# Layers 2 and 3 of a four-layer network on one core: columns in natural order, one load per pair half, six input and output buffers, rounding and residual copy on GpSimd

## The chip, the cores and the metric

The kernel runs on one core of one Trainium2 chip. The time is the device time of one execution in microseconds. A core has five engines with a queue of instructions each: PE multiplies matrices, DVE (VectorE), ACT (ScalarE) and POOL (GpSimd) work on tiles in the core's memory, and SP (SyncE) here only issues transfers. Each engine takes its instructions in a fixed order, and an instruction that waits holds up all that is behind it. Transfers between the chip's main memory and the core run on 16 DMA engines, whichever queue issues them. Matmul results arrive in PSUM, a second, small memory[...]. Tiles have 128 partitions.

## What is computed

The input x is (4, 8, 512, 512) in float32: 4 images, 8 channels, 512 rows, 512 columns. Four layers follow each other. Each normalizes x over groups of two channels and adds a function of the result to x:

```python
def _gn(v, G=4, eps=1e-5):          # mean and variance over 2 channels and all pixels
    ...
x = x + _L0_conv_ref(_gn(x), ...)   # spiking attention
x = x + _L1_conv_ref(_gn(x), w)     # 13 x 13 blur of each channel
x = x + _L2_conv_ref(_gn(x), weight, bias)
x = x + _L3_conv_ref(_gn(x), weight, bias)

def _L2_conv_ref(x, weight, bias):  # quantized 3 x 3 convolution over 8 channels
    sx = MAX_Q / jnp.max(jnp.abs(x))
    sw = MAX_Q / jnp.max(jnp.abs(weight))
    qx, qw = _quantize(x, sx), _quantize(weight, sw)     # round and clip to +-127
    out_i32 = lax.conv_general_dilated(qx, qw, ...)
    return out_i32 / (sx * sw) + bias[None, :, None, None]
```

Layer 3 is an ordinary float32 3 x 3 convolution over 8 channels with a bias. The change touches layers 2 and 3 alone.

## The kernel before

Layer 0 and layer 1 run first and take most of the time. Layer 1 leaves its result in main memory as `x2d[t]`, one array for each image t, with a row for each image row and channel. The columns of such a row don't lie in natural order there: they lie by phase, which means that column 4 v + g stands at place 128 g + v (`PH` = 4 phases, `NV` = 128 columns of each). The layers 2 and 3 of the kernel before keep this order to the end.

`layers23` works on windows of 8 image rows by 8 channels, 64 partitions each; a window advances by 6 rows. Two windows make a tile of 128 partitions by 512 columns (`windows(k)`), two tiles make a pair, and an image has 22 pairs, so 88 pairs in all. A 3 x 3 convolution is three matmuls for each window, one for each column offset dx; the rows and channels are in the band matrix. In the phase order, the neighbouring column of phase 3 is in phase 0 of the next v, so the tiles carry two more phases at their ends (`PH + 2`), which `outer_phases` fills by two shifted copies on POOL (L931, L932).

For a pair, `layer2` does this:
- `load(t, p)` (L936): four transfers of 128 KB on SP's queue, one for each window of each tile (L941), into a tile `x` out of a pool of four (L220). The loop asks for the load three pairs ahead (L1076).
- L951, ACT: y = x times scale plus bias, the normalization and the quantization scale.
- L956, DVE: rounding of y to whole numbers by adding and subtracting 12582912, written as bf16 to one of three tiles `xq`.
- L931 and L932, POOL: the outer phases of `xq`.
- L968, PE: 12 bf16 matmuls, 64 x 64 weights on 64 x 512 columns.
- L973, DVE: x3 = result times `inv` plus x (the residual, read from the loaded tile), into a ring `x3` of 24 pairs that stays in the core's memory; L976, DVE: its statistics.

After 11, 19 and 22 pairs of an image, `halos` copies border rows between windows inside `x3` (L993 on SP; L995 on SP, or on POOL's queue for the last chunk of an image). After 22 pairs `norm3` works out the normalization of layer 3 from the statistics: short DVE instructions, small matmuls and a power on POOL (L191).

`layer3` runs 23 pairs behind: L931 and L932 fill the outer phases of the pair in `x3`, L1039 (POOL) sets the two border columns, L1046 is 24 float32 matmuls, L1056 (ACT) adds the bias and writes the result `o` with the columns put back into natural order (it reads PSUM with a stride of 128 elements), into a pool of three. L1067 stores it, 192 KB: the first tile of a pair from ACT's queue, the second from POOL's.

The order within each queue comes from the framework's scheduler, which works at build time with estimated durations; `issue_after(did)` only asks that PE take a pair's layer 3 after the layer 2 of the current step. A pair's steps are thus not one after another: while PE works on one pair, ACT and DVE can be at later ones, as far as buffers (x 4, y 2, xq 3, PSUM 3 and 4, o 3) let them.

Of the kernel before, what the change touches and what calls it, by code (L numbers as in the profile page):

```python
# [42 lines left out]
P = 128  # L43
# [82 lines left out]
def network(ctx: ExitStack, tc: tile.TileContext, i: dict, out: bass.AP):  # L126
# [84 lines left out]
    def pool(name, bufs=1, **where):  # L211
# [5 lines left out]
    r2 = late.tile([P, T, G], F32, name="r2")  # L217
    most = late.tile([P, G], F32, name="most")
    early = {
        "x": ctx.enter_context(pool("x2", 4, side="right")),  # L220
        "y": ctx.enter_context(pool("y2", 2, side="right")),
        "o": ctx.enter_context(pool("o3", 3, side="right")),
    }
    with ExitStack() as s:
        ps_1 = s.enter_context(pool("ps_2", space=PSUM))
# [573 lines left out]
def weights23(tc, i, pool, scratch, ps_1, ident):  # L799


    nc = tc.nc

    def col(name, n=1):
        return pool.tile([P, n], F32, name=name)

    n_taps = 3 * B
    w = {}
    c24 = pool.tile([n_taps, i["c24"].shape[1]], F32, name="c24")
    nc.scalar.dma_start(c24, i["c24"])  # L810
    w2 = pool.tile([n_taps, n_taps], F32, name="w2t")
    nc.scalar.dma_start(w2, i["w2"])
    w3 = pool.tile([n_taps, n_taps], F32, name="w3t")
    nc.scalar.dma_start(w3, i["w3"])
    w["b2"], b3 = col("b2"), col("b3")
    nc.scalar.dma_start(w["b2"], i["b2"])
    nc.scalar.dma_start(b3, i["b3"])
    w["b23"] = col("b23")
    nc.vector.tensor_add(w["b23"], w["b2"], b3)

    def banded(taps, dtype, name, firsts):

        band = pool.tile([P, len(firsts), 3, HALF], dtype, name=name)
        for b, first in enumerate(firsts):
            ps = ps_1.tile([P, W_IN, n_taps], F32, tag="misc", name=f"ps_{name}")
            for row in range(W_IN):
                at = (W_IN - first - row) * B
                for a in range(2):
                    nc.tensor.matmul(
                        ps[a * HALF : (a + 1) * HALF, row, :], lhsT=c24[:, at : at + HALF],  # L830
                        rhs=taps, start=True, stop=True,
                    )
            for dx in range(3):
                nc.vector.tensor_copy(
                    band[:, b, dx, :].rearrange("p (r c) -> p r c", c=B),
                    ps[:, :, dx * B : (dx + 1) * B],
                )
        return band

    w["band3"] = band3 = banded(w3, F32, "band3", (-1, 1))
    w["sum3"] = pool.tile([P, 2, HALF], F32, name="sum3")
    nc.vector.tensor_add(w["sum3"], band3[:, :, 0, :], band3[:, :, 1, :])
    nc.vector.tensor_add(w["sum3"], w["sum3"], band3[:, :, 2, :])
    w["eye3"] = pool.tile([P, 2, 3, HALF], F32, name="eye3")
    nc.vector.memset(w["eye3"], 0.0)
    nc.vector.tensor_add(
        w["eye3"][:, 0, 1, B:], ident[:, : HALF - B], ident[:, HALF : P - B]
    )  # L850
    nc.vector.tensor_add(
        w["eye3"][:, 1, 1, : HALF - B], ident[:, B:HALF], ident[:, HALF + B :]
    )

    wall = scratch.tile([P, 2, D], F32, tag="y", name="wall")
    wall = wall.rearrange("p n d -> p (n d)")[:, : n_taps * n_taps]
    nc.scalar.dma_start(wall, bass.AP(i["w2"].tensor, 0, [[0, P], [1, n_taps * n_taps]]))
    w["sw"] = sw = col("sw")
    nc.vector.tensor_reduce(sw, wall, AX.X, ALU.max, apply_absolute_value=True)
    nc.vector.reciprocal(sw, sw)  # L860
    nc.vector.tensor_scalar_mul(sw, sw, MAX_Q)
    nc.vector.tensor_scalar_mul(w2, w2, sw[:n_taps])
    nc.vector.tensor_scalar(w2, w2, MAX_Q, -MAX_Q, op0=ALU.min, op1=ALU.max)
    nc.vector.tensor_scalar(w2, w2, ROUND, ROUND, op0=ALU.add, op1=ALU.subtract)
    w["band2"] = banded(w2, BF16, "band2", (0,))


    w["xq"] = [pool.tile([P, 2, PH + 2, NV], BF16, name=f"xq_{j}") for j in range(3)]
    for xq in w["xq"]:
        nc.gpsimd.memset(xq, 0.0)  # L870
    w["st3"] = [pool.tile([P, W2_N, 6], F32, name=f"st3_{j}") for j in range(2)]
    for st3 in w["st3"]:
        nc.gpsimd.memset(st3, 0.0)
    w["inv"] = col("inv")
    w["m"], w["r"] = col("m_own", T), col("r_own", T)
    w["mr"] = col("mr_own", T)
    return w


def layers23(  # L880
# [33 lines left out]
        w["mr"], w["m"], -1.0, w["r"], op0=ALU.mult, op1=ALU.mult  # L914
    )

    x3p = s.enter_context(pool("x3"))

    x3 = x3p.tile([P, 2 * RING, PH + 2, NV], F32, name="x3")
    flat = x3.rearrange("p n g v -> p n (g v)")  # L920
    last = (PH + 2) * NV - 1
    nc.gpsimd.memset(flat[:, :, 0 : last + 1 : last], 0.0)
    def tiles(p):
        return [k for k in (2 * p, 2 * p + 1) if k < W2_N]

    def slot(t, p):
        return 2 * ((t * N_PAIRS + p) % RING)

    def outer_phases(x):

        nc.gpsimd.tensor_copy(x[:, :, 0, 1:], x[:, :, PH, : NV - 1])  # L931
        nc.gpsimd.tensor_copy(x[:, :, PH + 1, : NV - 1], x[:, :, 1, 1:])  # L932

    ahead = {}

    def load(t, p):  # L936
        ahead[t, p] = xt = early["x"].tile([P, 2, D], F32, tag="x", name=f"x2_{t}_{p}")
        src = x2d[t]
        for j, k in enumerate(tiles(p)):
            for a, q in windows(k):  # L940
                nc.sync.dma_start(  # L941
                    xt[a * HALF : (a + 1) * HALF, j, :],
                    bass.AP(src.tensor, src.offset + q * W_STEP * B * D, [[D, HALF], [1, D]]),
                )

    def layer2(t, p):
        ks = tiles(p)
        n, n_p = len(ks), HALF * len(windows(ks[-1]))
        xt = ahead.pop((t, p))
        y = early["y"].tile([P, 2, D], F32, tag="y", name="y2")  # L950
        nc.scalar.activation(  # L951
            y[:n_p, :n, :], xt[:n_p, :n, :], AF.Identity, bias=w["mr"][:n_p, t : t + 1],
            scale=w["r"][:n_p, t : t + 1],
        )
        xq = w["xq"][(t * N_PAIRS + p) % 3][:n_p, :n]
        nc.vector.tensor_scalar(  # L956
            xq[:, :, 1 : PH + 1, :], y[:n_p, :n, :].rearrange("p n (g v) -> p n g v", g=PH),
            ROUND, ROUND, op0=ALU.add, op1=ALU.subtract,
        )
        outer_phases(xq)  # L960
        s0 = slot(t, p)
        st3 = w["st3"][t % 2]
        for j, k in enumerate(ks):
            ps = ps_2.tile([P, D], F32, tag="conv2", name="ps_conv2")
            for dx in range(3):
                for a, _ in windows(k):
                    half = slice(a * HALF, (a + 1) * HALF)
                    mm = nc.tensor.matmul(  # L968
                        ps[half, :], lhsT=w["band2"][half, 0, dx, :], rhs=xq[half, j, dx : dx + PH, :],
                        start=dx == 0, stop=dx == 2,  # L970
                    )
            own = x3[:n_p, s0 + j, 1 : PH + 1, :].rearrange("p g v -> p (g v)")
            nc.vector.scalar_tensor_tensor(  # L973
                own, ps[:n_p, :], w["inv"][:n_p], xt[:n_p, j, :], op0=ALU.mult, op1=ALU.add
            )
            nc.vector.bn_stats(st3[:n_p, k, :], own)  # L976
        return mm.ins

    pairs = flat[:, :, NV : (PH + 1) * NV].rearrange("p (n j) d -> p n j d", j=2)

    def halos(t, p0, p1):


        for c in range(4):
# [4 lines left out]
            for q0, q1, n_q in split(t, first, n, before - 1):  # L989
# [1 line left out]
                there = pairs[a_b * HALF : (a_b + 1) * HALF, q1 : q1 + n_q, j_b, :]  # L991
                end = (W_IN - 1) * B
                nc.sync.dma_start(here[:B], there[W_STEP * B : (W_STEP + 1) * B])  # L993
                engine = nc.gpsimd if p1 == N_PAIRS else nc.sync
                engine.dma_start(there[end : end + B], here[B : 2 * B])  # L995

    def split(t, p, n, back):

# [32 lines left out]
    def layer3(t, p, zero, band, const):  # L1031
# [2 lines left out]
        ks = tiles(p)  # L1034
        s0 = slot(t, p)
        n_p = HALF * len(windows(ks[-1]))
        outer_phases(x3[:n_p, s0 : s0 + len(ks)])
        edge = flat[:n_p, s0 : s0 + len(ks), 0 : last + 1 : last]
        nc.gpsimd.tensor_copy(edge, zero[:n_p].unsqueeze(2).to_broadcast([n_p, len(ks), 2]))  # L1039
        ps = [ps_3.tile([P, D], F32, tag="conv3", name="ps_conv3") for _ in ks]  # L1040
        for dx in range(3):
            for j, k in enumerate(ks):
                for a, q in windows(k):
# [1 line left out]
                    b = 1 if q == W_ALL - 1 else a ^ j  # L1045
                    nc.tensor.matmul(  # L1046
                        ps[j][b * HALF : (b + 1) * HALF, :], lhsT=band[half, b, dx, :],
                        rhs=x3[half, s0 + j, dx : dx + PH, :],
                        start=dx == 0, stop=dx == 2,
                    )  # L1050
        for j, k in enumerate(ks):
            q = 4 * p + 2 * j
            used = slice(HALF if q == W_ALL - 1 else 0, P)

            o = early["o"].tile([P, D], F32, tag="o", name="o3")
            nc.scalar.activation(  # L1056
                o[used].rearrange("p (v g) -> p v g", g=PH),
                ps[j][used].rearrange("p (g v) -> p v g", g=PH), AF.Identity, bias=const[used],
            )
            row, n = q * W_STEP + 1, 2 * W_STEP  # L1060
            at = 2 * B
            if q == 0:
                row, n, at = row - 1, n + 1, at - B
            if q == W_ALL - 1:
                n, at = W_STEP + 1, HALF
            engine = nc.gpsimd if j else nc.scalar
            engine.dma_start(  # L1067
                out[t, :, row : row + n, :].rearrange("c r w -> r c w"), o[at : at + n * B, :]
            )
# [3 lines left out]
    n_all = T * N_PAIRS  # L1073
    for n in range(n_all + N_PAIRS + 1):
        if n < n_all:
            for m in range(4) if n == 0 else [n + 3]:  # L1076
                if m < n_all:
                    load(*divmod(m, N_PAIRS))
            t, p = divmod(n, N_PAIRS)
# [47 lines left out]
```

## Time and profile before

| | us |
|---|---|
| median of 3 runs | 3185.09 |
| lowest and highest | 3183.04, 3185.96 |
| the profiled execution | 3180.31 |
| its span, first to last instruction | 3178.2 |
| layers 2 and 3 in it, from the first L951 at 2595.9 to the end | 582.3 |

All times of single steps come from the profiled execution. Over the whole span PE is busy 92%, DVE 70%, POOL 31%, ACT 15%. This is an average over stages. The page's 40 slices, each 79.5 us long, show it; a digit is the busy share of a slice in tenths:

```profile
PE   8999999999999999999999999989999974757778
DVE  5997698688688779779768868864555566545550
ACT  1300000010010000000000001001111121434443
POOL 1241243234333333134224323331111122343332
PEclk9999999999999999999999999989999986889899
DMA  5222222222222221212111111138877754656664
```

PE is nearly full until slice 33, that is to the end of layer 1. From there, where layers 2 and 3 are, the digits of PE fall to 4 to 8, and no other row takes its place at 9. The clock that PE is granted falls too.

### The profile page before, as it was taken

To read this page: it belongs to the slowest core of one execution; us is meant where nothing else is said; L and a number is where in the kernel's file an instruction comes from. 1 tells how busy PE (TensorE), PEld (TensorE's weight loads), DVE (VectorE), ACT (ScalarE), POOL (GpSimd) and SP (SyncE) were. 2 spreads that over 40 slices of the span, in tenths; PEclk is the share of its full clock that TensorE was granted. 3 is DMA by queue.
4 is the path that set the end of the run, shared out by engine and by line. 5 is a ranking of instruction groups with operands and counts; after the bars stand their busy time and mean duration, and the time that the engine had idled before them with its cause. 6 is when DMAs were issued, how large, how long until landed. Compare 5 with 4: busy or idle time off the path is not lost. (4 is left out here: it accounts for less than half of the span.)

```text
span 3178.2 us, 38965 instructions
## 1 busy us (share of the span) xinstructions
PE 2939.1 (92%) x13993; PEld 1483.4 (47%) x13993; DVE 2233.5 (70%) x3761; ACT 486.6 (15%) x657; POOL 970.4 (31%) x2150
## 2 busy tenths in 40 slices
PE   8999999999999999999999999989999974757778
PEld 6555555555555555555555555543333322323333
DVE  5997698688688779779768868864555566545550
ACT  1300000010010000000000001001111121434443
POOL 1241243234333333134224323331111122343332
PEclk9999999999999999999999999989999986889899
DMA  5222222222222221212111111138877754656664
GB/s 177 77 81 69 66 68 68 67 67 68 64 67 72 65 64 61 80 61 68 61 54 48 54 48 54 38 94 204 218 207 206 219 138 109 169 155 186 165 163 123
DMA packets 275255, 327.37 MB, mean 103 GB/s; under 512 B 24848, under 2 KB 172440, under 8 KB 274837
## 3 DMA queue, kind: packets, MB, share of 16 engines
q1 hardware_dynamic: 202154, 212.64, 24.8%
q0 software_dynamic: 23744, 68.43, 6.4%
q10 hardware_dynamic: 49163, 43.81, 4.6%
q8 instruction: 109, 1.79, 0.2%
q14 instruction: 85, 0.70, 0.1%
HBM read 210.60 MB, written 103.17 MB: 99 GB/s over the span
## 5 line engine op out<-in xcount | busy, mean ns | idle before, releaser
L451 PE MATMUL ps_in<-w_v,xn 128*128 128x512 f32 x1024 | 461.9, 600 | 2.4 <-issue 2.1
L451 PE MATMUL ps_in<-w_k,xn 128*128 128x512 f32 x1024 | 450.2, 592 | 1.1 <-DVE v_k L416 0.8
L451 PE MATMUL ps_in<-xn,w_q 128*128 128x512 f32 x1024 | 449.6, 592 | 0.1
L737 PE MATMUL ps_conv<-x,bt 112*64 112x512 f32 x2048 | 444.2, 593 | 0.0
L487 PE MATMUL ps_b<-toep,vtok 128*64 128x512 bf16 x3072 | 370.1, 381 | 0.0
L536 POOL COPY x1s<-x1s 128x2 f32<-128x2 f32 (+1 forms) x1024 | 227.8, 282 | 296.0 <-DVE x1s L525 296.0
L514 PE MATMUL ps_out<-wp,so 128*128 128x512 f32 x1024 | 308.9, 444 | 0.0
L399 ACT ACTIVATE h_q<-v_q,c_half 128x512 f32<-128x512 f32 x96 | 69.3, 722 | 1543.5 <-DVE v_q L395 1260.1
L1046 PE MATMUL ps_conv<-x,band_t 64*64 64x512 f32 x2040 | 280.4, 610 | 23.4 <-ACT o L1056 15.5
L424 POOL TENSOR_TENSOR h_v<-h_v,c_v 128x512 f32<-128x512 f32 x96 | 123.2, 1283 | 576.2 <-DVE h_v L423 541.6
L451 PEld LDWEIGHTS ps_in<-w_k,xn 128*128 128x128 f32 x1024 | 194.1, 190 | 222.5 <-issue 204.3
L451 PEld LDWEIGHTS ps_in<-xn,w_q 128*128 128x128 f32 x1024 | 191.8, 190 | 220.0 <-issue 213.1
L451 PEld LDWEIGHTS ps_in<-w_v,xn 128*128 128x128 f32 x1024 | 190.3, 191 | 216.7 <-issue 211.2
L968 PE MATMUL ps_conv<-xq,band 64*64 64x512 bf16 x1020 | 154.9, 436 | 140.8 <-POOL xq L931 127.6
L737 PEld LDWEIGHTS ps_conv<-x,bt 112*64 112x64 f32 x2048 | 150.2, 135 | 285.4 <-issue 284.4
L487 PEld LDWEIGHTS <-vtok 128*64 128x64 bf16 x3072 | 208.9, 110 | 122.9 <-issue 1.7
L514 PEld LDWEIGHTS ps_out<-wp,so 128*128 128x128 f32 x1024 | 192.6, 188 | 94.1 <-issue 58.3
L525 DVE SCALAR_TENSOR_TENSOR x1s<-v_p,xr 128x256 f32<-128x256 f32 x256 | 186.6, 769 | 15.2 <-DMA x<-x1s 3.9
L968 PEld LDWEIGHTS <-band 64*64 64x64 bf16 x1020 | 78.9, 121 | 226.9 <-issue 203.1
L753 POOL DMA_DIRECT2D x<-xo x128 | 71.6, 566 | 359.0 <-ACT xo L744 344.6
L1046 PEld LDWEIGHTS ps_conv<-x,band_t 64*64 64x64 f32 x2040 | 119.3, 136 | 128.0 <-issue 83.2
L424 POOL TENSOR_TENSOR h_k<-h_k,c_k 128x512 f32<-128x512 f32 x96 | 124.5, 1297 | 117.5 <-DVE h_k L423 117.5
(178 smaller groups left out, 3513.1 us busy)
## 6 DMA issues: line engine op xcount, KB each, us to landing
x<-x SPq DMA_DIRECT2D x64, 917.0 KB
x<-x SPq DMA_DIRECT2D x374, 128.0 KB
x<-x1s POOLq DMA_DIRECT2D x128, 262.0 KB, 2.6
x<-in_x SPq DMA_DIRECT2D x128, 256.0 KB
xr<-in_x SPq DMA_DIRECT2D x128, 256.0 KB
xs<-in_x SPq DMA_DIRECT2D x112, 256.0 KB
x<-xo ACTq DMA_DIRECT2D x128, 128.0 KB
x<-xo POOLq DMA_DIRECT2D x128, 128.0 KB, 5.9
```

The lines of the kernel that those rows point to most:

```text
L399: nc.scalar.activation(h, v, AF.Identity, bias=c_col, scale=0.5)
L424: nc.gpsimd.tensor_add(h, h, c_twice[n])
L451: mm = nc.tensor.matmul(ps, lhsT=lhsT, rhs=rhs, start=k == 0, stop=k == NC - 1)
L487: nc.tensor.matmul(pb[two * DH : (two + 1) * DH, :], lhsT=v[:, c, h * DH : (h + 1) * DH], rhs=toep[z][:, h, u : u + N], start=c == 0 and z ...
L514: nc.tensor.matmul(ps, lhsT=so[:, k, c * P : (c + 1) * P], rhs=wpT[z][:, k, :], start=k == 0 and z == 0, stop=k == NC - 1 and z == 1,)
L525: nc.vector.scalar_tensor_tensor(own, v.rearrange("p (g v) -> p g v", g=PH)[:, two, :], 1.0, by_phase[:, two, :], op0=ALU.is_ge, op1=ALU.add,)
L536: nc.gpsimd.tensor_copy(x1[:, f, u : u + n], x1[:, fm, um - n + 1 : um + 1][:, ::-1])
L737: nc.tensor.matmul(ps[q * M1 : (q + 1) * M1, :], lhsT=bt[:, z, :], rhs=xt[:, w0 : w0 + N_PS1, z : z + NV], start=z == 0, stop=z == SHIFTS - 1,
L753: engine.dma_start(bass.AP(dst.tensor, dst.offset + (q * n_half * W1_OUT * B + b) * D + f * NV, [[B * D, W1_OUT], [W1_OUT * B * D, n_half] ...
L968: mm = nc.tensor.matmul(ps[half, :], lhsT=w["band2"][half, 0, dx, :], rhs=xq[half, j, dx : dx + PH, :], start=dx == 0, stop=dx == 2,)
L1046: nc.tensor.matmul(ps[j][b * HALF : (b + 1) * HALF, :], lhsT=band[half, b, dx, :], rhs=x3[half, s0 + j, dx : dx + PH, :], start=dx == 0, s ...
```

## The change

The columns of layers 2 and 3 lie in natural order. The arrays in main memory that layer 1 writes stay in phase order; so the order is turned where a tile is read. Part by part:

- The load of a pair is one transfer for each window position a that covers both tiles, so two transfers of 256 KB in place of four of 128 KB.
- The pool of x has six tiles, and the loop asks for loads five pairs ahead. The pool of o has six tiles.
- A new tile `u` (pool of three) holds the residual in natural order: a POOL copy that reads x with a stride of 128 elements. L973 reads `u` in place of x.
- L951 reads x with the same stride, and writes y in natural order.
- The rounding is on POOL, in place of DVE.
- `outer_phases` is gone with its four copies a pair; the tiles have one border column at each side instead, which matmuls read at offsets of one element.
- L1056 reads and writes in natural order.
- The second store of a pair and all halo copies are on SP's queue, in place of POOL's.

```diff
-        "x": ctx.enter_context(pool("x2", 4, side="right")),
+        "x": ctx.enter_context(pool("x2", 6, side="right")),
+        "u": ctx.enter_context(pool("u2", 3, side="right")),
         "y": ctx.enter_context(pool("y2", 2, side="right")),
-        "o": ctx.enter_context(pool("o3", 3, side="right")),
+        "o": ctx.enter_context(pool("o3", 6, side="right")),
...
-    w["xq"] = [pool.tile([P, 2, PH + 2, NV], BF16, name=f"xq_{j}") for j in range(3)]
+    w["xq"] = [pool.tile([P, 2, D + 4], BF16, name=f"xq_{j}") for j in range(3)]
...
-    x3 = x3p.tile([P, 2 * RING, PH + 2, NV], F32, name="x3")
-    flat = x3.rearrange("p n g v -> p n (g v)")
-    last = (PH + 2) * NV - 1
-    nc.gpsimd.memset(flat[:, :, 0 : last + 1 : last], 0.0)
+    x3 = s.enter_context(pool("x3")).tile([P, 2 * RING, D + 2], F32, name="x3")
...
-    def outer_phases(x):
-
-        nc.gpsimd.tensor_copy(x[:, :, 0, 1:], x[:, :, PH, : NV - 1])
-        nc.gpsimd.tensor_copy(x[:, :, PH + 1, : NV - 1], x[:, :, 1, 1:])
...
-        for j, k in enumerate(tiles(p)):
-            for a, q in windows(k):
-                nc.sync.dma_start(
-                    xt[a * HALF : (a + 1) * HALF, j, :],
-                    bass.AP(src.tensor, src.offset + q * W_STEP * B * D, [[D, HALF], [1, D]]),
-                )
+        first, second = (dict(windows(k)) for k in (2 * p, 2 * p + 1))
+        for a, q in first.items():
+
+            n = 2 if a in second else 1
+            step = second[a] - q if n == 2 else 1
+            nc.sync.dma_start(
+                xt[a * HALF : (a + 1) * HALF, :n, :],
+                bass.AP(
+                    src.tensor, src.offset + q * W_STEP * B * D,
+                    [[D, HALF], [step * W_STEP * B * D, n], [1, D]],
+                ),
+            )
...
+        def own_order(x):
+            return x[:n_p, :n, :].rearrange("p n (g v) -> p n v g", g=PH)
+
+        def by_unit(x):
+            return x[:n_p, :n, :].rearrange("p n (v g) -> p n v g", g=PH)
+
+        u = early["u"].tile([P, 2, D], F32, tag="u", name="u2")
         y = early["y"].tile([P, 2, D], F32, tag="y", name="y2")
+        nc.gpsimd.tensor_copy(by_unit(u), own_order(xt))
         nc.scalar.activation(
-            y[:n_p, :n, :], xt[:n_p, :n, :], AF.Identity, bias=w["mr"][:n_p, t : t + 1],
+            by_unit(y), own_order(xt), AF.Identity, bias=w["mr"][:n_p, t : t + 1],
             scale=w["r"][:n_p, t : t + 1],
         )
         xq = w["xq"][(t * N_PAIRS + p) % 3][:n_p, :n]
-        nc.vector.tensor_scalar(
-            xq[:, :, 1 : PH + 1, :], y[:n_p, :n, :].rearrange("p n (g v) -> p n g v", g=PH),
-            ROUND, ROUND, op0=ALU.add, op1=ALU.subtract,
-        )
-        outer_phases(xq)
+        nc.gpsimd.tensor_scalar(
+            xq[:, :, 2 : D + 2], y[:n_p, :n, :], ROUND, ROUND, op0=ALU.add, op1=ALU.subtract
+        )
...
-                        ps[half, :], lhsT=w["band2"][half, 0, dx, :], rhs=xq[half, j, dx : dx + PH, :],
+                        ps[half, :], lhsT=w["band2"][half, 0, dx, :], rhs=xq[half, j, dx + 1 : dx + 1 + D],
...
-                own, ps[:n_p, :], w["inv"][:n_p], xt[:n_p, j, :], op0=ALU.mult, op1=ALU.add
+                own, ps[:n_p, :], w["inv"][:n_p], u[:n_p, j, :], op0=ALU.mult, op1=ALU.add
...
-                engine = nc.gpsimd if p1 == N_PAIRS else nc.sync
-                engine.dma_start(there[end : end + B], here[B : 2 * B])
+                nc.sync.dma_start(there[end : end + B], here[B : 2 * B])
...
-        outer_phases(x3[:n_p, s0 : s0 + len(ks)])
-        edge = flat[:n_p, s0 : s0 + len(ks), 0 : last + 1 : last]
+        edge = x3[:n_p, s0 : s0 + len(ks), 0 : D + 2 : D + 1]
         nc.gpsimd.tensor_copy(edge, zero[:n_p].unsqueeze(2).to_broadcast([n_p, len(ks), 2]))
...
-                        rhs=x3[half, s0 + j, dx : dx + PH, :],
+                        rhs=x3[half, s0 + j, dx : dx + D],
...
-            nc.scalar.activation(
-                o[used].rearrange("p (v g) -> p v g", g=PH),
-                ps[j][used].rearrange("p (g v) -> p v g", g=PH), AF.Identity, bias=const[used],
-            )
+            nc.scalar.activation(o[used], ps[j][used], AF.Identity, bias=const[used])
...
-            engine = nc.gpsimd if j else nc.scalar
+            engine = nc.sync if j else nc.scalar
...
-            for m in range(4) if n == 0 else [n + 3]:
+            for m in range(6) if n == 0 else [n + 5]:
```

## The prediction

> **What bounds the kernel now.** First the busy time by stretch of time, over the part the change touches: layers 2 and 3, from 2595.9 us (the first L951) to the end of the span.
>
> ```profile
> 2595.00:2712.00 117.00, 48.33 (x264) 24.75 (x265) 77.76 (x128) 28.21 (x24) 35.22 (x95) 0.66 0.47 112
> 2712.00:3104.00 392.00, 280.47 (x2315) 145.46 (x2314) 218.19 (x363) 161.75 (x194) 144.60 (x396) 0.88 0.62 167
> 3104.00:3178.20 74.20, 63.82 (x514) 25.66 (x514) 0.84 (x3) 28.93 (x43) 20.75 (x55) 0.96 0.44 123
> ```
>
> The columns are PE, PEld, DVE, ACT, POOL, granted clock, DMA share, GB/s. In stretch 1 (layer 2 of t = 0 alone, 22 pairs) nothing is busy; in stretch 2 (layer 2 beside layer 3 of the image before, 65 pairs) PE is 72% busy, DMA 62%; only stretch 3 (layer 3 alone) is near PE's limit. Next, who waits (first three lines: 2700 to 3000 us; last: SP's queue, 2590 to 2712), and the chain of waits where it ran unhindered:
>
> ```profile
> ACT y L951 <- DMA x<-x: 84.4, 37, 21.4
> PE ps_conv L968 <- POOL xq L931: 58.0, 15, 13.5
> ACT o L1056 <- DMA out<-o: 53.2, 22, 5.9
> ...
> SPq L941 <- DVE x L973: 56.8, 9, 36.8
> ...
> 3003.85 1.08 PE ps_conv L968 x10
> 3005.14 2.57 PE ps_conv L1046 x22
> 3007.72 1.08 PE ps_conv L968 x10
> ```
>
> ACT waits for loads, because a load waits for one of four x buffers, held until L973 has added the residual; and it waits for stores, because there are three o buffers. PE's wait for POOL is the end of that chain: load, L951, L956, L931. When fed, a pair takes PE 3007.72 - 3003.85 = 3.87 us; the mean in stretch 2 is near 6. So the bound is two buffer rings, not an engine. Last, what a step costs, from the groups by shape (2580 to 3180 us, then the two L36x lines from layer 0):
>
> ```profile
> L973 DVE SCALAR_TENSOR_TENSOR x<-ps_conv,inv,x 128x512 f32<-128x512 f32 x168 | 119.4, 742 | 37.1 <-PE ps_conv L968 32.3 <-DMA x<-x 4.7
> L1056 ACT ACTIVATE o<-ps_conv,const 128x512 f32<-128x512 f32 x168 | 113.1, 683 | 170.1 <-DMA out<-o 103.4 <-PE ps_conv L1046 27.7 <-ACT o L1056 20.3
> L976 DVE BATCH_NORM_STATS2 st<-x 128x6 f32<-128x512 f32 x168 | 108.3, 680 | 0.2
> L951 ACT ACTIVATE y<-x,mr_own,r_own 128x1024 f32<-128x1024 f32 x84 | 103.7, 1239 | 185.7 <-DMA x<-x 164.7 <-DVE mr_own L913 9.2 <-DVE xq L956 6.4
> L956 DVE TENSOR_SCALAR xq<-y 128x1024 bf16<-128x1024 f32 x84 | 63.8, 763 | 128.3 <-ACT y L951 126.1 <-POOL xq L931 1.0 <-POOL xq L932 0.9
> L931 POOL COPY x<-x 128x254 f32<-128x254 f32 x84 | 33.4, 398 | 22.6 <-DMA x<-x 22.6
> L931 POOL COPY x<-x 64x127 f32<-64x127 f32 x4 | 1.1, 284 | 0.0
> ...
> L362 DVE SCALAR_TENSOR_TENSOR wp_k<-wp,cols,scale_p 128x512 f32<-128x512 f32 x4 | 4.7, 1191 | 0.0
> L367 DVE TENSOR_TENSOR wp_k<-wp_k,wp 128x512 f32<-128x512 f32 x4 | 3.0, 760 | 0.0
> ```
>
> The two copy lines give GpSimd's rate: (398 - 284) / 127 = 0.90 ns an element, plus 0.17 us. L362 reads 512 columns with a stride of 16 bytes, L367 without: (1191 - 760) / 512 = 0.84 ns more an element.
>
> **What the Trainium skill says.** (1) GPSIMD Engine Reference, sections 3.1 and 7: a light one-input body runs at 1.03 cycles an element at 1.2 GHz (0.86 ns; the trace's 0.90 agrees), but a read with a step over 8 bytes costs about 2.9 cycles in place of 1.9; no strided GpSimd stream is in this trace. (2) SBUF — State Buffer, "Door 1: The DMA port swizzle": the memory has 16-byte lines and a new line at each access costs; the L362 line agrees for DVE. (3) The same page, "Who interferes with whom": a two-port DVE instruction (tensor_scalar can be one) shuts GpSimd out while it runs. The trace agrees: the L932 copy of xq takes a median of 402 ns, but 0.98 us at 2608.68, when an L956 starts at 2608.73. (4) TensorE: Matmul & The Clock Gate, "What's actually happening": after idling PE runs at half clock. The trace agrees: 12 L968 take 2.77 us at 2715.42, after 9.95 us idle, while 10 take 1.27 us when warm.
>
> **The change part by part,** per pair.
> *Removed.* DVE's L956, 0.76 us: DVE falls from 2 x (0.742 + 0.680) + 0.763 = 3.61 to 2.84 us. Four L931/L932 copies on POOL, 4 x 0.40 to 0.43 = 1.65 us, and POOL's store issue, 0.57 us. None is a bound where loads stall, so alone each gives little; the copies' 0.8 us leave the chain load to matmul.
> *Added on POOL.* A residual copy of 1024 elements, read with a stride of 512 bytes. Low end, as if packed: 0.17 + 1024 x 0.90 ns = 1.09 us; with L362's surcharge 1.95; high end, the skill's 2.9 cycles: 2.47 + 0.17 = 2.64. I take 2.2. The rounding, packed: 1.09 us, or 1.79 at 1.9 cycles; I take 1.1, as two simple operations. With 0.15 of gaps POOL needs 3.45 us a pair, and 3.65 with L1039's edge copy (0.195). A gain is excluded: the copies are new work. In order on POOL the rounding stands behind the residual copy, which waits for the load and for a u buffer (freed by L973 three pairs back); matmul L968 waits for the rounding.
> *ACT.* L951 now reads with that stride. L1056 reads PSUM with it today and takes 683 ns, against 688 for the unstrided L744, so PSUM shows no surcharge; for SBUF nothing is shown. Low end 1.24 us, high 1.24 + 1024 x 0.84 ns = 2.10; I take the high one, since the line rule held on DVE. ACT then needs 2.10 + 2 x 0.68 + one store issue of 0.79 (the issue holds up the next ACTIVATE in the trace) + 0.15 = 4.4 us, above PE's 3.87. L1056 becoming unstrided gains nothing, by the same comparison.
> *SP.* Four load issues of about 0.6 us become two; one store (0.79) comes, and the halo issues that POOL had (16 in all). Under 2.5 us a pair. A store on SP waits for L1056 and the loads behind it wait too; POOL's longest such wait was 6.6 us, against five pairs (over 19 us) loaded ahead, so it is hidden; without that cover it costs its whole length.
> *Rings.* x is freed by L951 and the residual copy, not by L973, and is six deep: the loop issue 1.3 + landing 4.5 (once 7.9) + reading 2.2 = 8 us over six pairs, 1.3 us a pair: not late any more. o at six: the store waits (up to 8.5 us) spread over three pairs, 2.8 us. DMA: 896 KiB a pair; 167 GB/s at share 0.62 extrapolates to 269 GB/s, 3.4 us. What is late next is ACT, then PE, POOL and DMA close behind.
> *PE.* The same matmuls, now at offsets of one element. In f32 this is free (L737 shifts, 593 ns; L451 doesn't, 592 to 600). For bf16 not shown: nothing, up to 8 of 12 passes doubled, +0.86 us; I take nothing.
>
> Sum. Of 2595.9 to 3178.2 = 582.3 us. Stretch 1: 22 x 3.45 (POOL) = 76, lead-in 4, norm boundary 8. Stretch 2: 65 x 4.4 = 286, two boundaries at 4 (they stalled PE 7 to 10 us, in good part on loads queued behind halos on SP). Stretch 3: 23 pairs; PE's 63.8 us plus norm and tail, 68 (it waits 26 us on stores now, most beside PE). Total 76 + 286 + 88 = 450, a saving of 132. Span 3178 - 132 = 3046; 2.1 around it gives 3048; the median of runs stands 4.8 above the profiled execution (3180.3), so **3053**.
>
> **The rivals.** *No surcharge on strides*: PE and DVE bound. 22 x 2.85 + 65 x 3.95 + 82 = 401: 3004. For: PSUM reads; against: L362. *GpSimd at its high ends*: 2.64 + 1.79 + 0.15 = 4.6 in stretch 1, with the edge 4.9: 101 + 318 + 88 = 507, 3110; doubled bf16 passes (4.75) land near it. *The wait moves to SP*: stores ahead of loads hold the ring as o did, 5.2 us a pair: 76 + 338 + 88 = 502, 3105. Against: the depth. *GpSimd becomes the bound, slower*: from 87 p + 88 = 582 the break-even is p = 5.7 us, that is copy and rounding together above 5.3 us. L424 shows a two-input GpSimd rate of 1283 ns for 512, 2.17 ns an element: rounding at that rate 2.39, the copy at that rate plus the stride 3.25, with gaps and edge 6.0: 87 x 6.0 + 88 = 610, about 3213. For: nothing in the trace shows a two-operation or strided stream on GpSimd. Against: both have one input.
>
> **How the numbers follow.** ACT-bound 0.50 (own range 3025 to 3080), no surcharge 0.22, GpSimd high 0.14, SP 0.05, slower 0.09. The range 3000 to 3125 leaves out the slower case and tails. A change within 0.2% (6.4 us) can't be told from none: the cases that end there are a POOL period near 5.7, 0.02; slower 0.08; faster 0.90.
>
> **What would show it.** L951 at 2.1 us with ACT the busiest of stretch 2 (right), at 1.24 (second case). Copy plus rounding: 3.3 us; above 5.3 the sign is wrong. ACT's waits for loads and stores should fall from 164.7 and 103.4 us to a few tens; if they stay, the rings weren't the bound.

## The result and the profile after

The changed kernel is slower.

| | us |
|---|---|
| before, median of 4 runs (lowest, highest) | 3184.07 (3182.47, 3185.96) |
| after, median of 4 runs (lowest, highest) | 3271.85 (3270.23, 3278.45) |
| ratio, with its 95% interval | 1.0279 (1.0262 to 1.0297) |
| profiled execution after, and its span | 3270.23, 3268.5 |
| predicted | 3053, range 3000 to 3125 |

Layers 2 and 3 take 2595.4 to 3268.5 = 673 us instead of 582. Everything ahead of them is as it was. In the changed kernel the lines are renumbered: the load is L937, the residual copy L958, the normalization L959 (L951 of before), the rounding L964 (L956), the matmuls of layer 2 L974 (L968), the residual add L979 (L973), the halo copies L999 and L1000, the matmuls of layer 3 L1050 (L1046), the output L1059 (L1056), the store L1067.

Three rows of the page of the changed kernel, each digit a slice of 81.7 us:

```profile
PE   8999999999999999999999999999999745566668
POOL 1241342243243234333333233221111497787870
DMA  5222122222212222222111111187777653555554
```

In the last eight slices, but for the very last one, POOL, which stood at 2 to 4 there before, is at 7 to 9, PE at 4 to 6, and DMA, mostly 6 there before, mostly at 5. One engine, POOL, has taken the place of the two rings. The busy time by stretch of the changed kernel, in the columns of before (PE, PEld, DVE, ACT, POOL, granted clock, DMA share, GB/s):

```profile
2595.00:2736.00 141.00, 61.46 (x287) 28.06 (x288) 65.92 (x111) 51.03 (x24) 126.66 (x63) 0.56 0.44 86
2736.00:3188.00 452.00, 290.40 (x2268) 135.65 (x2269) 173.47 (x277) 216.80 (x189) 354.18 (x181) 0.85 0.55 141
3188.00:3268.50 80.50, 68.19 (x549) 33.45 (x541) 4.70 (x16) 32.25 (x48) 3.59 (x23) 0.94 0.47 131
```

In stretch 1 (22 pairs of layer 2 alone) POOL is busy 127 of 141 us, 90%: it is the bound there. In stretch 2 (65 pairs, both layers) it is busy 354 of 452 us, 78%, and no other engine but PE passes a half. The last stretch, layer 3 alone, has hardly any work on POOL; from the last L974 it took 81 us, where the kernel before took 88 from its last L968, at 3090.0. What fills POOL, from the groups by shape of the changed kernel (2580 to 3270 us: busy us, mean ns, idle time before and what ended it):

```profile
L964 POOL TENSOR_SCALAR xq<-y 128x1024 bf16<-128x1024 f32 x84 | 305.5, 3639 | 21.6 <-ACT y L959 21.6
L959 ACT ACTIVATE y<-x,mr_own,r_own 128x1024 f32<-128x1024 f32 x84 | 182.8, 2183 | 156.5 <-POOL xq L964 103.3 <-DMA x<-x 43.9 <-DVE mr_own L914 9.2
L974 PE MATMUL ps_conv<-xq,band 64*64 64x512 bf16 x1020 | 167.0, 462 | 209.7 <-POOL xq L964 208.5 <-DVE x L979 0.9
L958 POOL COPY u<-x 128x1024 f32<-128x1024 f32 x81 | 160.3, 1979 | 75.8 <-DMA x<-x 75.8
```

The rounding takes 3.64 us on GpSimd. On VectorE (L956 before) it took 0.763. PE waits 208.5 us for it, ACT 103.3. How POOL runs when nothing holds it up, from the timeline of the changed kernel (start, duration):

```profile
2778.57 3.62 POOL L964 TENSOR_SCALAR xq<-y 128x1024 bf16<-128x1024 f32 x1
2782.15 1.98 POOL L958 COPY u<-x 128x1024 f32<-128x1024 f32 x1
2784.09 3.63 POOL L964 TENSOR_SCALAR xq<-y 128x1024 bf16<-128x1024 f32 x1
```

A pair takes 2784.09 - 2778.57 = 5.5 us, back to back. The mean in stretch 2 is 452 / 65 = 6.95, so POOL is not all of it. It is idle for 98 us of that stretch, and 70 of these are waits of the copy for its load. Where the loads are held up shows in SP's own queue (first POOL's wait in stretch 2, then SP's waits from 2580 to 3270 us: us in total, times, longest):

```profile
POOL u L958 <- DMA x<-x: 70.2, 11, 20.1
...
SPq L1067 <- ACT o L1059: 143.6, 44, 7.5
SPq L937 <- DMA out<-o: 54.8, 12, 24.5
SPq L937 <- ACT y L959: 37.5, 6, 30.7
```

Stores wait on SP for ACT, and the loads L937 stand behind them; loads also wait for earlier stores to land. At the end of the first image's layer 2, where eight halo issues come together, the timelines of SP, ACT and POOL in the changed kernel show this (all but the first of the halo issues left out; the line of waits is SP's from 2717 to 2747 us):

```profile
2706.47 0.74 SPq L999 DMA_DIRECT2D x<-x  x1
...
2717.26 29.87 SPq L937 DMA_DIRECT2D x<-x  x6
...
SPq L937 <- DMA out<-o: 24.5, 1, 24.5
...
2740.71 0.69 ACT L1059 ACTIVATE o<-ps_conv,const 128x512 f32<-128x512 f32 x1 [22.12 <-PE ps_conv L1050]
2741.43 0.89 ACTq L1067 DMA_DIRECT2D out<-o  x1
...
2742.95 2.13 ACT L959 ACTIVATE y<-x,mr_own,r_own 128x1024 f32<-128x1024 f32 x1
...
2745.17 3.63 POOL L964 TENSOR_SCALAR xq<-y 128x1024 bf16<-128x1024 f32 x1 [7.00 <-ACT y L959]
```

The halo issues hold SP for 10.8 us. The six load issues that follow are spread over 30 us, and 24.5 of these are one wait, for the store that ACT issues at 2741.43 to land. That store is on another queue. In layers 2 and 3 of this trace, every transfer of SP's and ACT's queues counts its landing on one of the same eight semaphores (counters that an issue can wait for), and each issue on SP waits until the transfer before it on its own semaphore has landed. This load shares one with that store, which came late because layer 3 began late. Transfers of POOL's queue, in the runs that have them in this part, count on eight others. L964's wait of 7.00 us has the same root: the L959 that it needs stands on ACT behind two L1059, the first of which had waited 22.12 us for layer 3's first matmuls.

### The profile page after: what moved, and what is told of

Same layout as the page of the kernel before. It is cut to its first block, busy times and chain, and to the rows that moved or that the text cites. A ratio compares the mean times of both kernels' runs of the same rounds, so it can differ in the third digit from the quotient of the medians.

```text
span 3268.5 us, 38350 instructions
## 1 busy us (share of the span) xinstructions
PE 2967.3 (91%) x13993; PEld 1484.3 (45%) x13993; DVE 2177.4 (67%) x3673; ACT 567.8 (17%) x657; POOL 1256.8 (38%) x1873
## 3 DMA queue, kind: packets, MB, share of 16 engines
q8 instruction: 109, 1.79, 0.2%
## 5 line engine op out<-in xcount | busy, mean ns | idle before, releaser
L974 PE MATMUL ps_conv<-xq,band 64*64 64x512 bf16 x1020 | 167.0, 462 | 209.7 <-POOL xq L964 208.5
L979 DVE SCALAR_TENSOR_TENSOR x<-ps_conv,inv,u 128x512 f32<-128x512 f32 (+1 forms) x172 | 123.9, 747 | 342.6 <-PE ps_conv L974 220.1
L1050 PE MATMUL ps_conv<-x,band_t 64*64 64x512 f32 x2040 | 300.1, 639 | 36.1 <-ACT o L1059 30.6
L964 POOL TENSOR_SCALAR xq<-y 128x1024 bf16<-128x1024 f32 x88 | 313.1, 3563 | 21.6 <-ACT y L959 21.6
L959 ACT ACTIVATE y<-x,mr_own,r_own 128x1024 f32<-128x1024 f32 x88 | 188.1, 2143 | 166.3 <-POOL xq L964 113.1
L974 PEld LDWEIGHTS <-band 64*64 64x64 bf16 x1020 | 77.7, 124 | 304.8 <-issue 283.6
L958 POOL COPY u<-x 128x1024 f32<-128x1024 f32 x88 | 170.8, 1942 | 86.7 <-DMA x<-x 86.7
```

What stands on the lines that cost most here:

```text
L958: nc.gpsimd.tensor_copy(by_unit(u), own_order(xt))
L959: nc.scalar.activation(by_unit(y), own_order(xt), AF.Identity, bias=w["mr"][:n_p, t : t + 1], scale=w["r"][:n_p, t : t + 1],)
L964: nc.gpsimd.tensor_scalar(xq[:, :, 2 : D + 2], y[:n_p, :n, :], ROUND, ROUND, op0=ALU.add, op1=ALU.subtract)
L974: mm = nc.tensor.matmul(ps[half, :], lhsT=w["band2"][half, 0, dx, :], rhs=xq[half, j, dx + 1 : dx + 1 + D], start=dx == 0, stop=dx == 2,)
L979: nc.vector.scalar_tensor_tensor(own, ps[:n_p, :], w["inv"][:n_p], u[:n_p, j, :], op0=ALU.mult, op1=ALU.add)
L1050: nc.tensor.matmul(ps[j][b * HALF : (b + 1) * HALF, :], lhsT=band[half, b, dx, :], rhs=x3[half, s0 + j, dx : dx + D], start=dx == 0, stop= ...
```

## The experiments

Each time is a median of its runs, each ratio one to executions of the kernel before on the same chip. The kernel before had medians of 3180.65, 3183.47, 3184.53 and 3186.24 in the four groups of runs.

| label | built on | edit | us | ratio (95%) |
|---|---|---|---|---|
| e1_round_dve | after | rounding back on DVE | 3162.37 | 0.9942 (0.9923 to 0.9961) |
| e2_before_round_pool | before | rounding on GpSimd | 3263.14 | 1.0257 (1.0231 to 1.0282) |
| e3_y_from_u | e1 | normalization reads u | 3175.46 | 0.9983 (0.9975 to 0.9991) |
| e4_small_rings | e1 | x 4 deep, o 3 deep | 3181.42 | 0.9998 (0.9988 to 1.0008) |
| e7_u_ring | e1 | u 6 deep | 3166.26 | 0.9943 (0.9923 to 0.9963) |
| e5_store_pool | e1 | second store on GpSimd's queue | 3136.98 | 0.9858 (0.9841 to 0.9875) |
| e8_halo_pool | e5 | halo copies on GpSimd's queue | 3115.71 | 0.9790 (0.9773 to 0.9807) |
| e9_halo_y_from_u | e8 | normalization reads u | 3201.51 | 1.0055 (1.0040 to 1.0070) |
| e10_y_from_u_ring | e9 | u 6 deep | 3143.23 | 0.9871 (0.9855 to 0.9888) |
| e12_halo_pool_u | e8 | u 6 deep | 3139.29 | 0.9850 (0.9834 to 0.9867) |
| e11_before_sp | before | second store and all halos on SP | 3198.58 | 1.0047 (1.0032 to 1.0062) |

**The rounding alone, taken out of the change and put into the kernel before.**

```diff
-        nc.gpsimd.tensor_scalar(
+        nc.vector.tensor_scalar(
             xq[:, :, 2 : D + 2], y[:n_p, :n, :], ROUND, ROUND, op0=ALU.add, op1=ALU.subtract
```

> The changed kernel with the rounding (L964) back on VectorE, all else as changed. Theory A (the rounding on GpSimd costs 3.6 us a pair in place of the 1.1 of the prediction, and with the 1.98 us copy makes GpSimd the bound at 5.8 us a pair): GpSimd falls to 2.2 us a pair, ScalarE at 2.18 + 2 x 0.68 + 0.8 = 4.4 us becomes the bound, and the time falls to 3050 to 3100 us, below the 3184 of the kernel before. Theory B (the loads that stand behind stores and halo copies on SP's queue, and the strided reads, are the bound): the time stays above 3200.

The same edit the other way round, on the kernel before:

> The kernel before with the rounding (L956) on GpSimd and nothing else changed. Theory A: one rounding lasts about 3.6 us, GpSimd needs 3.6 + 4 x 0.41 + 0.2 + 0.57 = 6.0 us a pair beside layer 3, and the time is 3215 to 3300. Theory B: 3180 to 3200, since the rest of the change, not the rounding, costs the time.

Measured: without it the changed kernel falls by 109.5 us, to 3162.37, 0.6% faster than before; with it alone the kernel before rises by 82.5 us, inside its range. Moving the rounding alone takes either kernel from the level of the kernel before, or a little below it, to well above it. No run has the rounding on GpSimd with the stores and halo copies off SP. The first run missed its own range, though: 3162 is well above 3100. Something else in the change costs. The waits of e1 (2590 to 3161 us) point to it:

```profile
POOL u L958 <- DMA x<-x: 163.4, 37, 27.0
...
POOL u L958 <- DVE x L979: 105.1, 47, 5.6
```

With POOL relieved, its copy waits 163 us for loads: the six-deep x ring does not bring the data in time. Its wait of 105 us for L979 is for a free u buffer.

**What the rounding costs on GpSimd, form by form.** The changed kernel, with its rounding still on GpSimd, and 4 x 9 extra GpSimd instructions on constant data after the last layer. The expectation names the kernel of e1 as its base; the one that ran is the changed kernel. Its time is compared with nothing.

```diff
+            nc.gpsimd.tensor_copy(f_out, f_in)
+            nc.gpsimd.tensor_copy(h_out, f_in)
+            nc.gpsimd.tensor_scalar(h_out, f_in, ROUND, ROUND, op0=ALU.add, op1=ALU.subtract)
+            nc.gpsimd.tensor_scalar(f_out, f_in, ROUND, ROUND, op0=ALU.add, op1=ALU.subtract)
+            nc.gpsimd.tensor_scalar(f_out, f_in, ROUND, None, op0=ALU.add)
...
+            nc.gpsimd.tensor_scalar(f_out[:, :1, :], f_half, ROUND, ROUND, op0=ALU.add, op1=ALU.subtract)
+            nc.gpsimd.tensor_scalar(f_out[:, :1, :], f_half, ROUND, None, op0=ALU.add)
+            nc.gpsimd.tensor_copy(f_out.rearrange("p n (v g) -> p n v g", g=PH), f_in.rearrange("p n (g v) -> p n v g", g=PH))
```

> The first experiment of this call, with 4 x 9 extra GpSimd instructions after the end of layer 3, which write tiles that nothing reads, to time their forms. Theory A1 (each arithmetic operation of a tensor_scalar costs): one operation takes about half of two, 3.6 us to about 1.9, whatever the output type. Theory A2 (the bf16 output costs): f32 output takes about 1.1 us with two operations, bf16 3.6. Theory A3 (the whole instruction is slow on this engine, a fixed cost an element): all four forms near 3.6 us for 1024 elements. A half-size one tells fixed cost from cost by element: 1.9 us if by element. The plain copy 1.1 us, the strided copy 1.9.

The groups of that kernel by shape; L249 and L250 have two operations, L251 one, L253 and L254 are two and one at half size, L247 and L248 are plain copies, L255 is the copy with the stride of L958:

```profile
L250 POOL TENSOR_SCALAR f_out<-f_in 128x1024 f32<-128x1024 f32 x4 | 14.5, 3636 | 0.2
L249 POOL TENSOR_SCALAR h_out<-f_in 128x1024 bf16<-128x1024 f32 x4 | 14.5, 3635 | 0.0
L251 POOL TENSOR_SCALAR f_out<-f_in 128x1024 f32<-128x1024 f32 x4 | 11.1, 2774 | 0.2
L253 POOL TENSOR_SCALAR f_out<-f_in 128x512 f32<-128x512 f32 x4 | 7.7, 1930 | 0.2
L255 POOL COPY f_out<-f_in 128x1024 f32<-128x1024 f32 x4 | 7.7, 1922 | 0.1
L254 POOL TENSOR_SCALAR f_out<-f_in 128x512 f32<-128x512 f32 x4 | 6.0, 1494 | 0.2
L248 POOL CAST h_out<-f_in 128x1024 bf16<-128x1024 f32 x4 | 4.2, 1041 | 0.0
L247 POOL COPY f_out<-f_in 128x1024 f32<-128x1024 f32 x4 | 4.2, 1038 | 0.1
```

None of the three theories held whole. The type of the output makes no difference (L249 against L250), as A1 said, but one operation takes 76% of the time of two, not half. Two operations cost (3636 - 1930) / 512 = 3.33 ns an element, one costs (2774 - 1494) / 512 = 2.50; a plain copy of the same size takes 1.04 us in all. So it isn't the second operation that makes the rounding dear; it adds 0.84 ns an element, a quarter. Already the first arithmetic operation takes 2.7 times a copy's time. The stride of L958 adds (1922 - 1038) / 1024 = 0.86 ns an element.

**The loads: ring depth or queue.** Built on e1. These four are one group of runs and e1 is of an earlier one; taken by the ratios, the differences from e1 below are 18, 0 and 27 us instead of 19, 4 and 25. First the depth: the rings cut back to those of before, with as many pairs loaded ahead as they allow.

```diff
-        "x": ctx.enter_context(pool("x2", 6, side="right")),
+        "x": ctx.enter_context(pool("x2", 4, side="right")),
-        "o": ctx.enter_context(pool("o3", 6, side="right")),
+        "o": ctx.enter_context(pool("o3", 3, side="right")),
...
-            for m in range(6) if n == 0 else [n + 5]:
+            for m in range(4) if n == 0 else [n + 3]:
```

> The kernel of the run e1_round_dve with the buffers of before: four x, three o, loads asked for three pairs ahead. The prediction's theory (the deeper rings carry the gain): 3230 us or more, since the waits of before for loads and stores come back. Rival (six of each can't be used, because SP's queue issues a load only when earlier transfers have landed): within 15 us of 3162.

Then u, from 3 buffers to 6, because POOL waited 105 us for one:

> The kernel of the run e1_round_dve with six residual tiles u in place of three. In stretch 1 of that run PE starts a new group of three pairs each 10.6 us, and GpSimd's copy L958 waits 105 us for L979 to free a u. Theory D (the u ring holds the rate in stretch 1 and part of stretch 2): 10 to 40 us less, and L958's wait for L979 gone. Theory C (loads late on SP): the wait moves to the loads, and the time stays within 8 us of 3162.

Then the second store of a pair, off SP:

```diff
-            engine = nc.sync if j else nc.scalar
+            engine = nc.gpsimd if j else nc.scalar
```

> The kernel of the run e1_round_dve (rounding on VectorE, 3162 us), and the second store of a pair (L1067) back on GpSimd's queue. Theory C (what is left of the loss to the prediction is SP's queue: loads stand behind stores that wait for ScalarE and behind the completion of earlier stores): the time falls by 20 to 60 us, to 3100 to 3140, and GpSimd's wait of L958 for loads falls from 163 us to under 100. Theory D (the buffers u and y and the strided ScalarE read hold the rate): within 10 us of 3162.

And the halo copies too:

```diff
-                nc.sync.dma_start(here[:B], there[W_STEP * B : (W_STEP + 1) * B])
-                nc.sync.dma_start(there[end : end + B], here[B : 2 * B])
+                nc.gpsimd.dma_start(here[:B], there[W_STEP * B : (W_STEP + 1) * B])
+                nc.gpsimd.dma_start(there[end : end + B], here[B : 2 * B])
```

> The kernel of the run e5_store_pool with all halo copies (L999, L1000) on GpSimd's queue too, so that only loads are left on SP. Theory C: the stalls of 9 to 19 us before L974 after each chunk of halos go, and the time is 20 to 60 us below that of e5_store_pool. Rival: the halo issues, some 126 of 0.57 us, now hold up the residual copies on GpSimd while they wait for L979 and for each other, and the time is the same or longer.

Measured: the small rings cost 19 us, between the two expectations and nearer the rival's; the u ring is worth nothing there (+3.9 us); the store on another queue gives 25.4 us, the halos another 21.3. e8 goes beyond undoing the change, since 110 of its 126 halo issues were on SP in the kernel before too. In e5 L958's wait for loads had fallen from 163.4 to 58.8 us; in e8 it is the last of these lines, the waits of e8 (2590 to 3113 us):

```profile
POOL out L1067 <- ACT o L1059: 127.5, 63, 5.7
...
DVE x L979 <- POOL u L958: 41.6, 8, 9.7
...
PE ps_const L1029 <- DVE scaled L1025: 29.0, 3, 11.1
...
POOL u L958 <- DMA x<-x: 15.6, 4, 9.8
```

So the loads were late because of the transfers in front of them, more than for want of buffers. Whether these held them up by their place on SP or by the shared semaphores was not separated, since a transfer that goes to POOL's queue leaves both. The semaphores do count: in e5, with no store left on SP, the loads there wait longer for stores to land than in e1 (the line is of e5, 2590 to 3270 us; e1 has 42.3 us, e8 1.8):

```profile
SPq L937 <- DMA out<-o: 71.9, 18, 16.4
```

The stores' wait for ACT is still there (127.5 us in e8), now on POOL, where the rounding no longer is. It delays the copies behind it; DVE's L979 waits 41.6 us for those. e8 is the fastest version: 3115.71 us, 2.1% below the kernel before and 156 us below the changed one. In an undisturbed piece of its timeline ACT is the bound that was predicted:

```profile
2739.63 2.22 ACT L959 ACTIVATE y<-x,mr_own,r_own 128x1024 f32<-128x1024 f32 x1
2741.75 0.68 ACT L1059 ACTIVATE o<-ps_conv,const 128x512 f32<-128x512 f32 x1
2742.45 0.78 ACTq L1067 DMA_DIRECT2D out<-o  x1
2743.34 0.69 ACT L1059 ACTIVATE o<-ps_conv,const 128x512 f32<-128x512 f32 x1 [0.91 <-PE ps_conv L974]
2743.92 2.22 ACT L959 ACTIVATE y<-x,mr_own,r_own 128x1024 f32<-128x1024 f32 x1
```

From one L959 to the next is 4.29 us. (The 0.91 in the last brackets is the store's issue, seen as idle time of ACT.)

**SP's part alone, on the kernel before.**

```diff
-                engine = nc.gpsimd if p1 == N_PAIRS else nc.sync
+                engine = nc.sync
...
-            engine = nc.gpsimd if j else nc.scalar
+            engine = nc.sync if j else nc.scalar
```

> The kernel before with one part of the change alone: the second store of a pair and all halo copies on SP's queue. Theory C (stores and halos in front of loads on SP cost time by themselves): 10 to 60 us slower than before, with ScalarE's wait of L951 for loads (165 us before) longer. Rival (they cost only beside the other parts): within 8 us of before.

Measured: +14.0 us (3198.58 against 3184.53). The step costs by itself too, but not by the wait that was expected to grow: ACT's wait for loads went from 164.7 us to 169.7 only. What grew is the wait of POOL's L931 for the copies inside x3, the halos (e11, 2580 to 3200 us; 22.6 us in the kernel before):

```profile
POOL x L931 <- DMA x<-x: 80.8, 14, 16.3
```

The 14.0 us can't be set against the 47 of e5 and e8 together, because e11 adds 16 halo issues to SP and e8 takes all 126 away.

**Shortening ACT.** If ACT is the bound at 4.4 us, reading u, which the copy has already put in order, should save about 0.9 us a pair:

```diff
-            by_unit(y), own_order(xt), AF.Identity, bias=w["mr"][:n_p, t : t + 1],
+            y[:n_p, :n, :], u[:n_p, :n, :], AF.Identity, bias=w["mr"][:n_p, t : t + 1],
```

> The first experiment of this call, and ScalarE's y is computed from the reordered copy u in place of a second strided read of x. If ScalarE's strided read (2.18 us in place of 1.24) sets the period once the rounding is away, this is faster than that experiment by up to 65 x 0.5 = 30 us, down to PE's 3.9 us a pair: 3020 to 3060. If ScalarE has slack there, the two are within 8 us of each other.

> The kernel of the run e8_halo_pool (3116 us), with ScalarE's y computed from the residual copy u in place of the strided x. In that run PE's steps repeat each 4.3 us in undisturbed stretches, which is ScalarE's 2.2 + 2 x 0.68 + 0.8: if the strided read on ScalarE sets this period, it falls towards PE's 3.9 and the time by 10 to 25 us, to 3090 to 3106. If the longer chain (copy, then y, then rounding) weighs more, as in the run e3_y_from_u, the time is the same or up to 20 us longer.

> The same with six tiles u: the copy can then run further ahead, and y after it. If u, now held from the copy to L979 and needed for y as well, is what makes the chain of that kernel long, 10 us or more below e9_halo_y_from_u; else within 8 us of it.

None is a gain: +13 us on e1, +86 on e8, and with six u buffers still +27.5 on e8. e3 and e9 lie outside both outcomes that were named for them; e10, 58 us below e9, is the outcome that its expectation names if the u buffers make the chain long. L959 did become shorter, 1.24 us (e3). But in e9 its longest wait is this:

```profile
ACT y L959 <- POOL u L958: 238.1, 77, 19.8
```

and POOL's timeline in e9 shows why the copy was late:

```profile
2752.24 0.57 POOL L1067 DMA_DIRECT2D out<-o  x1 [3.75 <-ACT o L1059]
2752.80 1.97 POOL L958 COPY u<-x 128x1024 f32<-128x1024 f32 x1
2758.52 0.57 POOL L1067 DMA_DIRECT2D out<-o  x1 [3.75 <-ACT o L1059]
```

POOL takes its instructions in order. The store waits 3.75 us for ACT's output, the copy stands behind the store, and ACT now waits for the copy: a loop of 6.3 us in place of 4.3. More u buffers, with which the copy can run further ahead, won 58 of the 86 us back. In e8 the normalization reads x, and ACT is in no such loop.

**More u buffers for the best version.**

> The kernel of the run e8_halo_pool (3116 us) with six residual tiles u in place of three. With the loads out of the way, the u ring should now decide stretch 1, where PE starts three pairs each 10.6 us: if so, 5 to 20 us less than e8_halo_pool. If ScalarE's 4.3 us and the norm boundaries carry the rest, within 5 us of it.

Measured: +23.6 us, a miss. PE waits 49.0 us, three times, for the small border copies L1043 on POOL, against 2.2 in e8. The trace of e12 shows two things at the longest of these waits, 21.5 us up to 2962.95. POOL runs six L958 in a row from 2949.69 to 2961.57, with single L1043 between them. And DVE, beside these copies, takes 10.95 us for one rounding (the one before took 0.68), after which the normalization goes on:

```profile
2951.22 10.95 DVE L964 TENSOR_SCALAR xq<-y 128x1024 bf16<-128x1024 f32 x1 [9.45 <-ACT y L959]
2962.09 0.60 DVE L1021 SCALAR_TENSOR_TENSOR band_t<-band,grstd_x,eye 128x384 f32<-128x384 f32 x1
```

No run with another order on POOL tested how much of the 23.6 us this is.

## Why the prediction was wrong

*The step that failed: "I take 1.1, as two simple operations".* The rounding measured 3.64 us, above even the bound of 1.79. The slower rival had the place and the break-even right: copy and rounding together above 5.3 us turn the sign, and they measured 1.98 + 3.64 = 5.62. That its own 3.25 + 2.39 = 5.64 is so near is luck: its copy was 1.27 us too long and its rounding 1.25 too short. Put into the prediction's own sum, with the medians and its 0.15 of gaps, POOL needs 1.96 + 3.62 + 0.15 = 5.73 us a pair in stretch 1 and 5.93 in stretch 2 with L1043: 22 x 5.73 + 65 x 5.93 + 88 = 599 us instead of 450. With the 5.5 us that POOL in fact takes back to back, and 0.2 for L1043, it is 22 x 5.5 + 65 x 5.7 + 88 = 580. So that one term is 130 to 149 of the 223 us by which layers 2 and 3 missed. It used up the whole gain, since the kernel before takes 582. The rest of the 223 came on top; POOL's waits for loads, 70 us in stretch 2, are its largest part. Taking the rounding off GpSimd moved the time by 109.5 us in the changed kernel.

Why it was mis-sized: the nearest row, the L931 copies, was a copy, and I read its rate as that of any light one-input stream. The Trainium skill (GPSIMD Engine Reference, section 3.1), which says 1.03 cycles an element for up to two operations, supported that. At the 1.2 GHz of that page the runs show 3.0 cycles for one operation (2.50 ns) and 4.0 for two (3.33 ns); the measurement decides. The two-input row L424, at 2.17 ns an element, was the nearest one with arithmetic in it, and it was used for the rival only.

*The residual copy.* 2.2 taken, 1.98 measured; "with L362's surcharge 1.95" was nearly exact, and 2.64, from 2.9 cycles an element, was too long. (The rival with GpSimd at its high ends also has a slip: its terms give 4.8 us with the edge, not 4.9, and so 3104 instead of 3110.)

*ACT.* 2.10 for L959 by carrying VectorE's surcharge over, 2.18 measured, and 4.4 us a pair, 4.29 in e8: right, though covered by POOL in the changed kernel. Some of it is luck, since L362 is another kind of instruction than L367, with two inputs read at a stride, and its stride is 16 bytes.

*SP: "so it is hidden"* was wrong. Taking the store and the halo issues off SP gave 25.4 and 21.3 us (e5, e8; most of the halos were on SP before the change too). Counting the issues' durations missed that an issue that waits holds all behind it: SP waited 143.6 us for L1059 alone. Five pairs loaded ahead would cover one wait of 7 us, but eight halo issues and then six load issues, one of which waits 24.5 us for a store on ACT's queue, 40 us together, use the cover up. That queues share semaphores was not in the prediction.

*Rings: "not late any more"* held for the buffers and not for the data. ACT's waits did fall as forecast, from 164.7 us to 43.9 for loads and from 103.4 to 42.9 for stores, in a kernel that became slower. Six-deep rings were worth 19 us (e4, with the rounding on DVE and the loads still behind stores on SP).

*PE at an offset of one bf16 element: nothing.* L974 has a median of 377 ns, L968 had 376: right.

*What is still open.* e8 takes 515 us (its first L959 at 2598.8, its end at 3113.5) where the sum had 450. Its windows put 105 us in stretch 1 (88 predicted), 331 in stretch 2 (294) and 79 in stretch 3 (68). PE's wait for L1025 at the three norm boundaries is 29.0 us, where the sum had 16, so 13 of the 65 us too much are there. The timeline of e8 at the first of them:

```profile
2696.05 6.16 DVE L1021 SCALAR_TENSOR_TENSOR band_t<-band,grstd_x,eye 128x384 f32<-128x384 f32 x1 [4.60 <-POOL grstd_x L191]
...
2702.33 0.38 PE L1029 MATMUL ps_const<-scaled,sum 64*64 64x1 f32 x4 [11.07 <-DVE scaled L1025]
```

L191, on POOL, stands behind the halo issues (4.6 us), and L1021 takes 6.16 us (its median over four is 6.14) where it takes 0.62 in the changed kernel, beside L958 copies that run from 2695.97 on. In stretch 1 DVE is the busiest engine, 85 of 105 us, with L964 at 1.21 us on average beside the copies. The rest of the 65 us was not traced to one cause, and a version with the boundary's work moved ahead of the halos was not tried.

## What to carry to other kernels

Before moving elementwise work to GpSimd, time the very form of instruction there: a copy's rate says nothing of an arithmetic one, which took 2.7 to 3.5 times as long on the same data. A queue that prefetches should hold nothing that waits for compute, and it is worth looking at whose landings its issues wait for; deeper rings bought less here than taking stores and halo copies out of the loads' way. And a shorter instruction on the bounding engine is no gain if its new input comes from an in-order queue that waits for that same engine.

## What the runs showed of the hardware

- GpSimd's tensor_scalar on 128 x 1024 f32: 3.64 us with two operations, 2.77 with one, against 1.04 for a copy or a cast; bf16 or f32 output alike. VectorE did the two operations in 0.76 us.
- ACT pays for a 512-byte stride in SBUF: 1.24 to 2.18 us for 1024 elements, 0.92 ns each, as GpSimd does (0.86) and VectorE with a 16-byte stride (0.84, from two different instructions). For the same stride in PSUM no cost was seen: L1056 with it and L1059 without it both take 683 ns.
- VectorE and GpSimd disturb one another. The rounding on VectorE took 1155 ns on average in e1 and 763 before. In e1, the 28 that ran with no GpSimd compute instruction beside them had a median of 694 ns, the other 56 of 1528; in e12 one took 10.95 us beside six copies in a row. L1021, with two SBUF inputs, took 6.16 us in e8 beside three such copies. The Trainium skill (SBUF — State Buffer, "Who interferes with whom") says that such an instruction contends with a GpSimd one that reads SBUF; this trace agrees, and the factor here was ten.
- Queues are coupled by the semaphores that their transfers count on: in the changed kernel SP's and ACT's queues share eight in layers 2 and 3, and a load on SP waited 24.5 us for a store on ACT's queue.
